# Four layers of graph networks with residuals on one core: W2·a kept in PSUM for the dots, and layer 3's statistics from ScalarE's sums

## The chip, the core and the metric

The kernel runs on one core of a Trainium2 chip. A core has five engines that work side by side, each through a queue of its own: TensorE (PE in the profile; its weight loads, PEld, overlap its products), VectorE (DVE), ScalarE (ACT), GpSimd (POOL) and SyncE (SP, which only starts transfers here). Data lies in SBUF; TensorE writes its results into PSUM, of which the kernel has eight banks of 128 partitions x 512 floats. Engines wait for each other only where one needs what another has written, or a buffer that another still reads.

The metric is the device time of one execution, in microseconds (us). The kernel before takes 2239.06 us, the median of three executions (2235.84 to 2239.59).

## The reference

The input x has 128 batches of 128 nodes with 512 features, all in fp32. Each of four layers adds its output to x and normalises over the features. Shapes and weights' names are cut here; `LN` is the normalisation without weights.

```python
# layer 0
y = einsum('nm,bmd->bnd', adj, x)
x = LN(x + einsum('bnd,do->bno', y, weight) + bias)
# layer 1
q, k, v = x @ Wq.T, x @ Wk.T, x @ Wv.T
rel = adj.T * einsum('bnd,bmd->bnm', q, k)
rel = rel / norm(rel, axis=2)
x = LN(x + einsum('bnm,bmd->bnd', rel, v))
# layer 2
h = x @ W                                # W is W2 in the kernel
s1, s2 = h @ a[:512], h @ a[512:]
e = leaky_relu(s1[:, :, None] + s2[:, None, :], 0.2) * adj
x = LN(x + elu(softmax(e) @ h + beta * h))
# layer 3: A = adj x, C = adj x + b, so C - A = b
out = max over the features of relu(A + b)      # one number per node
x = LN(x + out)
```

## The kernel before

**Tiling.** Four batches make a group, and there are 32 groups (G and NG). All four layers of a group are done on the core, so a group is loaded once and stored once. Large products, of 512 nodes x 512 by 512 x 512, are done with seven half-size products instead of eight (lines 290 to 362): y's product with layer 0's weights, m = x·(Wqᵀ·Wk) and v in layer 1, z in layer 2. Each of them runs seven steps in the order 1, 2, 6, 5, 7, 3, 4, and a step is eight matmuls of 256 columns. The running sums live in three PSUM tiles, r0, r1 and r2, each as large as a bank: r0 opens at step 1, r1 at step 2, r2 at step 5 (REGION, line 291). After a step its sum is read out, by a ScalarE copy or by a VectorE addition: in m, the copies are tT<-r_m after steps 1, 6, 5 and 4, and the additions tT<-r_m,tT after steps 2, 7 and 3. GpSimd makes the sums of left factors that the steps need (s_y, s_x, s_z; lines 294 to 311).

**Order.** Every engine runs in exactly the order in which the program names its instructions (InOrder, lines 18 to 26; since this helper records every operation, all rows of the profile say L26). The order is written out by hand: every piece of work has a due time, in 28 slots per group (TABLE, lines 231 to 246), and the pieces of all groups are sorted by due time (line 783) before they are emitted. A piece of group g that is due at 51.7 lies at 28·g + 51.7, so the four layers of neighbouring groups run interleaved: while layer 2 of a group is done, layer 0 of a later one is. FIRST (line 248) and LAST (lines 250 to 279) give other times to the first two and the last three groups.

**Around the change.** wa holds two rows, W2·a1 and W2·a2, spread over all partitions in SBUF (lines 138 and 202 to 212): since h·a = x·(W2·a), the reference's s1 and s2 are dot products of x rows with wa. VectorE does these dots on the unnormalised x2, two for each batch (line 559, scr<-x,wa, with the sum as a second output), and scale_dots (line 574, the instructions d) corrects them with the mean and the inverse deviation of the normalisation. Then TensorE spreads d (p_s, line 617) and the attention of layer 2 begins. The residual of layer 1 ahead of the dots (line 545, x<-p_o,rn,x) is followed by its statistics (stats, line 368: bn_stats and bn_aggr on VectorE). norm (line 375) is: VectorE adds eps (ve), GpSimd takes the power -0.5 (rstd), VectorE makes -mean·rstd (nmean), and ScalarE applies x·rstd + nmean.

In layer 3 (line 747) TensorE makes p_a = adj·x for a batch (widen), VectorE takes its greatest value over the features (mx), adds b and clips at zero (top), ScalarE adds that number to x, and then the statistics of this sum come from VectorE (stats3) and the norm follows.

**Buffers.** PSUM has one pool with two rings of four banks (lines 80 to 83): "ps" for single-bank tiles (p_y, p_rel, p_o, p_s, p_eT, p_z, p_a) and "r" for r0, r1, r2 of all products and, in the last group, for c (line 700). A matmul that opens a tile waits until the tile four before it in its ring has been read.

Of the kernel before, what the change touches and what calls it, by code (L numbers as in the profile page):

```python
# [8 lines left out]
FP = mybir.dt.float32  # L9
AF = mybir.ActivationFunctionType  # L10
ALU = mybir.AluOpType
AX = mybir.AxisListType

EPS = 1e-5
# [15 lines left out]
def kernel(  # L30
# [33 lines left out]
    pe, dve, act, pool = (InOrder(tc, e) for e in (nc.tensor, nc.vector, nc.scalar, nc.gpsimd))  # L64
    sync = InOrder(tc, nc.sync)
    B, N, D = x.shape
    P = 128
# [3 lines left out]
    H = D // 2  # L71
    G = 4
# [3 lines left out]
    const = ctx.enter_context(tc.tile_pool(name="const", bufs=1))  # L76
    data = ctx.enter_context(tc.tile_pool(name="data", bufs=2))
    work = ctx.enter_context(tc.tile_pool(name="work", bufs=1))
    small = ctx.enter_context(tc.tile_pool(name="small", bufs=4))
    psum = ctx.enter_context(tc.tile_pool(name="psum", bufs=4, space=bass.MemoryType.PSUM))  # L80

    def bank(name):
        return psum.tile([P, D], FP, tag="ps", name=name)

    def on_all(row, n):

# [5 lines left out]
    x1, x2, x3 = {}, {}, {}  # L92
# [28 lines left out]
    b3_sb = const.tile([P, 1], FP)  # L121
    nc.sync.dma_start(b3_sb, b3.rearrange("(p o) -> p o", o=1))

    ident = const.tile([P, P], FP)
    make_identity(nc, ident)
    mhalf = const.tile([P, G], FP)
    dve.memset(mhalf, -0.5)

    adjT = const.tile([P, P], FP)
    pt = bank("p_adjT")  # L130
    pe.transpose(pt[:, :P], adj_sb, ident)
    act.copy(adjT, pt[:, :P])
# [2 lines left out]

    m_qk = const.tile([P, K, D], FP)
    wvT = const.tile([P, K, D], FP)
    wa = const.tile([P, 2, D], FP)
    wa_sum = const.tile([P, 2], FP)
    beta_i = const.tile([P, P], FP)  # L140
    beta_b = beta_i[:, None, :].to_broadcast([P, G, P])
# [21 lines left out]
    def prepare_qk(c):  # L163

        pm = bank(f"p_m{c}")
        for e in range(K):
            pe.matmul(
                pm,
                wq_sb[:, e, c * P : (c + 1) * P],
                wk_sb[:, e, :],  # L170
                start=(e == 0),
                stop=(e == K - 1),
            )
        act.copy(m_qk[:, c, :], pm)
        if c == K - 1:
            bw["m"] = weight_blocks(m_qk, "m")
# [9 lines left out]
    col = const.tile([P, 2, K], FP)  # L186
# [15 lines left out]
    def prepare_rows():  # L202

        for i in range(2):
            p = bank(f"p_wa{i}")
            for k in range(K):
                pe.transpose(
                    p[:, k * P : (k + 1) * P], col[:, i, k : k + 1].to_broadcast([P, P]), ident
                )
            act.copy(wa[:, i, :], p)  # L210
        dve.tensor_reduce(wa_sum, wa, AX.X, ALU.add, negate=True)
        dve.tensor_scalar(beta_i, ident, beta_sb, None, op0=ALU.mult)

# [6 lines left out]
    def emit(at, f, *args):  # L220
        pieces.append((at, lambda: f(*args)))

    def each(at, f):
        for b in range(len(at)):
            emit(at[b], f, b)

    def row(at, step, n=G):
        return [at + i * step for i in range(n)]
# [6 lines left out]
        move=row(20.5, 0.1), x_sums=row(25.3, 0.5), m=row(28, 1, 7), scores=row(36.5, 1),  # L235
        masked=[39.95], squares=[40.4], turn_rel=[40.3],
        move_rel=row(41.2, 0.1), inverse=[42.5], v=row(42, 1, 7), attend=row(50.6, 1),
        residual=row(51.0, 1), dots=row(54.2, 1.1), norm1=[55.2], scale=[58.8],
        apply1=row(65.4, 0.33),
        spread=[61.6], leaky=[62.0], weighted=[63.4], greatest=[64.3], exps=[64.4],  # L240
        divide=[65.8], turn_att=[68.6], with_beta=[69.0], gather=row(71.5, 1),
# [2 lines left out]
        widen=[98.7, 100.0, 103.6, 104.6], top=[99.1, 100.4, 104.0, 105.0],  # L244
        stats3=[99.8, 101.1, 104.7, 105.7], norm3=[106.2], apply3=row(107, 0.33), store=[108.5],
# [8 lines left out]
            stats3=[27.0, 29.9, 32.2, 35.8], norm3=[42.0], apply3=row(44.0, 0.8), store=[47.4],  # L254
        ),
        NG - 2: dict(
            scale=[5.6], apply1=row(24.3, 0.8), spread=[6.9], leaky=[7.4], weighted=[9.0],
# [4 lines left out]
            top=[73.7, 74.6, 78.0, 78.9], stats3=row(79.8, 0.9), norm3=[83.4],  # L262
            apply3=row(84.8, 0.8), store=[88.2],
# [3 lines left out]
            squares=[17.2], turn_rel=[17.1], move_rel=row(18.0, 0.1), inverse=[20.0], v=[16.7, 18.4, 21.0, 22.7, 25.3, 27.9, 30.5],  # L267
            attend=row(33.2, 0.86), residual=row(34.1, 1.65), norm1=[40.65], dots=row(40.7, 1.53),
            scale=[47.0], apply1=row(47.5, 0.8), spread=[48.9], leaky=[49.4], weighted=[51.0],
# [5 lines left out]
            top=[83.5, 84.4, 85.3, 87.0], stats3=[86.1, 87.9, 88.8, 89.7],  # L275
            norm3=[86.9, 88.7, 89.6, 90.5], apply3=[88.3, 90.1, 91.0, 91.9],
# [62 lines left out]
    def product(at, name, mul, s, w, c, fresh, begin=None):  # L339


        r = {}

        def step(i):
            if i == 1 and begin is not None:
                begin()
            where = REGION[i]
            first = i in (1, 2, 5)
            if first:
                r[where] = psum.tile([P, 2, H], FP, tag="r", name=f"r{where}_{name}")  # L350
            mul(r[where], s["f"][i], bw[w][i], first)

        def out(i):
            p, dst = r[REGION[i]], c(*BLOCK[i])
            if fresh and i in (1, 6, 5, 4):
                act.copy(dst, p)
            else:
                dve.tensor_tensor(dst, p, dst, ALU.add)

        for n, i in enumerate(ORDER):  # L360
            emit(at[n], step, i)
            emit(at[n] + 0.72, out, i)
# [5 lines left out]
    def stats(s, g, b, t):  # L368
        if b == 0:
            s["mv"] = small.tile([P, G, 2], FP, tag="mv", name=f"mv_{g}", bufs=6)  # L370
        st = small.tile([P, 6], FP, tag="st", name=f"st_{g}_{b}")
        dve.bn_stats(st, t)
        dve.bn_aggr(s["mv"][:, b, :], st)

    def norm(at, apply_at, s, g, t):

        n = G // len(at)

        def spread(i):
            sl = slice(i * n, i * n + n)  # L380
            ve = small.tile([P, n], FP, tag=f"ve{n}", name=f"ve_{g}_{i}")
            dve.tensor_scalar(ve, s["mv"][:, sl, 1], EPS, None, op0=ALU.add)
            s["r", i] = small.tile([P, n], FP, tag=f"rstd{n}", name=f"rstd_{g}_{i}")
            pool.tensor_tensor(s["r", i], ve, mhalf[:, sl], ALU.pow)

        def shift(i):
            sl = slice(i * n, i * n + n)
            s["nm", i] = small.tile([P, n], FP, tag=f"nmean{n}", name=f"nmean_{g}_{i}")
            dve.scalar_tensor_tensor(
                s["nm", i], s["mv"][:, sl, 0], -1.0, s["r", i], op0=ALU.mult, op1=ALU.mult  # L390
            )

        def apply(b):
            i, j = b // n, b % n
            act.activation(
                t()[:, b, :],
                t()[:, b, :],
                AF.Identity,
                bias=s["nm", i][:, j : j + 1],
                scale=s["r", i][:, j : j + 1],  # L400
            )

        each(at, spread)
        for i in range(len(at)):
            emit(apply_at[i * n] - 0.1, shift, i)
        each(apply_at, apply)
# [207 lines left out]
    def layer2(g, t):  # L614
        s = {}
# [83 lines left out]

        def direct(b):  # L700

            s["c", b] = psum.tile([P, D], FP, tag="r", name=f"c_{g}_{b}")
            for k in range(K):
                pe.matmul(
                    s["c", b],
                    s["zT"][:, k, b * P : (b + 1) * P],
                    w2_sb[:, k, :],
                    start=(k == 0),
                    stop=(k == K - 1),
                )  # L710
# [15 lines left out]
        n = G // len(t["exps"])  # L726
# [20 lines left out]
    def layer3(g, t):  # L747
        s = {}

        def widen(b):  # L750
            s["a", b] = bank(f"p_a_{g}_{b}")
            pe.matmul(s["a", b], adjT, x3[g][:, b, :], start=True, stop=True)

        def top(b):
            x = x3[g][:, b, :]
            mx = small.tile([P, 1], FP, tag="mx", name=f"mx_{g}_{b}")
            dve.tensor_reduce(mx, s["a", b], AX.X, ALU.max)
            tp = small.tile([P, 1], FP, tag="top", name=f"top_{g}_{b}")
            dve.tensor_scalar(tp, mx, b3_sb, 0.0, op0=ALU.add, op1=ALU.max)
            act.activation(x, x, AF.Identity, bias=tp)  # L760

        def store(i):
            for b in range(i * n, i * n + n):
                sync.dma_start(out[g * G + b], x3[g][:, b, :])

        n = G // len(t["store"])
        each(t["widen"], widen)
        each(t["top"], top)
        each(t["stats3"], lambda b: stats(s, f"3_{g}", b, x3[g][:, b, :]))
        norm(t["norm3"], t["apply3"], s, f"3_{g}", lambda: x3[g])  # L770
        each(t["store"], store)


# [2 lines left out]
    each(row(18.0, 0.1), prepare_v)  # L776
    each(row(29.2, 1.8), prepare_dots)
    emit(40.7, prepare_rows)
    emit(61.0, prepare_2)
    for g in range(NG):  # L780
        for layer in (layer0, layer1, layer2, layer3):
            layer(g, times(g))
# [31 lines left out]
```

## Time and profile before

The profiled execution took 2236.61 us, and its span from first to last instruction is 2234.4 us. The mean granted TensorE clock is 0.996. The table gives busy time by stage: the filling of the pipeline, the main part with its regular groups, and the drain.

| stretch (us) | length | PE | DVE | ACT | POOL |
|---|---|---|---|---|---|
| 0 to 203 | 203.0 | 185.7 | 128.5 | 61.1 | 83.7 |
| 203 to 2100 | 1897.0 | 1887.1 | 1560.3 | 852.2 | 863.9 |
| 2100 to 2234.4 | 134.4 | 110.0 | 106.1 | 66.8 | 35.5 |

A busy time counts an instruction from start to end, so one that is held up by a neighbour in SBUF counts for longer. Groups of instructions are named by output and inputs: scr<-x,wa is the dot, tT<-r_m,tT an addition behind m's product. Some rows of the groups that the change touches (mean of one instruction, and the idle time of the engine right before it over the whole span):

| engine, instruction | count | mean ns | idle before, us |
|---|---|---|---|
| DVE mx<-p_a (128x512) | 128 | 677 | 7.6 |
| DVE top<-mx,b_sb | 128 | 215 | 4.6 |
| DVE mv<-st (bn_aggr) | 512 | 182 | 17.6 |
| DVE d<-mv,wa_sum,d | 64 | 450 | 0.0 |
| ACT x<-x,top (128x512) | 128 | 722 | 229.1 |
| ACT sq<-rel, square with sum (128x128) | 128 | 295 | 20.6 |
| ACT read of the accumulator behind it | 128 | 187 | 0.0 |
| POOL s_x<-xT (128x512 pieces) | 64 | 1497 | 256.5 |

### The profile page before, as it was taken

Reading aid. Unit: us, or ns where it says so; the run is one execution under the profiler, and the core shown is the slowest. Engines: PE = TensorE matmul, PEld = TensorE weight load, DVE = VectorE, ACT = ScalarE, POOL = GpSimd, SP = SyncE. Lnnn points to the kernel's source line nnn. Section 1 sums busy time; section 2 is a strip of 40 time slices with the busy share of each in tenths; the row PEclk is TensorE's granted clock in tenths of the full one; section 3 lists DMA queues with packets and bytes.
Section 4 is the critical chain, followed back from the end, with each engine's and each line's share of the span. In section 5 each row is a group of like instructions: output and inputs, shape, how many; then the busy total and the mean of one; then the engine's idle time right before and its main releaser. Section 6 shows DMA issues by size and latency. Waiting matters only on the chain.

```text
span 2234.4 us, 31661 instructions
## 1 busy us (share of the span) xinstructions
PE 2182.9 (98%) x11073; PEld 1842.1 (82%) x11073; DVE 1794.9 (80%) x3534; ACT 980.0 (44%) x1936; POOL 983.1 (44%) x743
## 2 busy tenths in 40 slices
PE   7999999999999999999999999999999999999996
PEld 5888888888888888888888888888888888888873
DVE  4668888778878788888788888788888788887788
ACT  2224444444444454444444444444344444444535
POOL 3435454435455344544344554344553354443322
PEclk9999999999999999999999999999999999999998
DMA  4010222211222211222201222202222112221101
GB/s 166 25 32 19 60 57 62 62 28 40 60 59 62 62 19 48 59 60 62 59 19 52 58 61 62 52 22 55 57 62 63 41 28 59 58 62 43 21 28 57
DMA packets 333294, 115.15 MB, mean 52 GB/s; under 512 B 297424, under 2 KB 297552, under 8 KB 333136
## 3 DMA queue, kind: packets, MB, share of 16 engines
q1 hardware_dynamic: 331936, 110.77, 19.6%
q10 hardware_dynamic: 1200, 2.36, 0.3%
q8 instruction: 89, 1.46, 0.3%
q14 instruction: 69, 0.57, 0.1%
HBM read 39.65 MB, written 33.55 MB: 33 GB/s over the span
## 4 chain that ended last, share of the span: by engine, by line
PE 75%; DVE 20%; issue 3%; POOL 1%; ACT 1%; DMA 0%; DVEq 0%; ACTq 0%; POOLq 0%
PE r_v L26 17%; PE r_y L26 15%; PE r_z L26 14%; PE r_m L26 8%; DVE scr L26 6%; DVE x L26 6%; PE p_z L26 5%; PE p_o L26 5%; PE p_a L26 5%; PE p_rel L26 4%; DVE st L26 2%; PE p_y L26 2%; DVE tT L26 1%; DVE d L26 1%; PE p_m L26 1%
## 5 line engine op out<-in xcount | busy, mean ns | idle before, releaser
L26 ACT ACTIVATE x<-x,nmean,rstd 128x512 f32<-128x512 f32 x512 | 385.8, 808 | 187.5 <-DVE nmean L26 187.4
L26 DVE BATCH_NORM_STATS2 st<-x 128x6 f32<-128x512 f32 x512 | 352.1, 688 | 56.7 <-ACT x L26 47.9
L26 DVE SCALAR_TENSOR_TENSOR scr<-x,wa 128x512 f32<-128x512 f32 x256 | 286.2, 1169 | 0.0
L26 POOL TENSOR_TENSOR rstd<-ve,mhalf 128x4 f32<-128x4 f32 (+1 forms) x134 | 145.2, 1083 | 286.9 <-DVE ve L26 280.7
L26 POOL TENSOR_TENSOR x<-x,bias_sb 128x512 f32<-128x512 f32 x128 | 193.2, 1519 | 76.9 <-PE p_y L26 76.4
L26 POOL TENSOR_TENSOR s_x<-xT 128x512 f32<-128x512 f32 x64 | 95.8, 1497 | 256.5 <-DMA xT<-xB 237.6
L26 ACT ACTIVATE x<-x,top 128x512 f32<-128x512 f32 x128 | 92.4, 722 | 229.1 <-DVE top L26 228.8
L26 DVE TENSOR_TENSOR x<-r_y,x 128x512 f32<-128x512 f32 x224 | 151.4, 676 | 27.1 <-PE r_y L26 27.0
L26 ACT COPY c<-r_z 128x512 f32<-128x512 f32 x124 | 71.8, 579 | 221.5 <-PE r_z L26 221.5
L26 ACT COPY yT<-p_y 128x512 f32<-128x512 f32 x128 | 75.1, 587 | 206.5 <-PE p_y L26 206.5
L26 PEld LDWEIGHTS p_y<-adjT,x 128*128 128x128 f32 x1024 | 135.8, 195 | 13.1 <-ACT adjT L26 5.2
L26 DVE SCALAR_TENSOR_TENSOR x<-p_o,rn,x 128x512 f32<-128x512 f32 x128 | 95.9, 749 | 59.9 <-PE p_o L26 56.0
L26 PE MATMUL p_y<-adjT,x 128*128 128x128 f32 x1024 | 136.7, 278 | 6.4 <-ACT adjT L26 4.9
L26 PEld LDWEIGHTS p_z<-eT,x 128*128 128x128 f32 x1024 | 133.9, 192 | 8.4 <-DVE x L26 1.2
L26 DVE SCALAR_TENSOR_TENSOR x<-m,x 128x512 f32<-128x512 f32 x128 | 129.7, 1013 | 13.6 <-DVE x L26 0.9
L26 PEld LDWEIGHTS p_rel<-xT,tT 128*128 128x128 f32 x1024 | 134.1, 191 | 7.4 <-DVE tT L26 0.8
L26 POOL TENSOR_TENSOR s_z<-zT 128x512 f32<-128x512 f32 x31 | 39.3, 1267 | 224.0 <-ACT zT L26 224.0
L26 PE MATMUL p_rel<-xT,tT 128*128 128x128 f32 x1024 | 134.9, 275 | 0.6 <-DVE tT L26 0.6
L26 PE MATMUL p_z<-eT,x 128*128 128x128 f32 x1024 | 134.8, 275 | 0.4 <-DVE x L26 0.4
L26 PE MATMUL p_a<-x,adjT 128*128 128x512 f32 x256 | 131.2, 597 | 3.6 <-ACT x L26 1.9
L26 ACT COPY tT<-r_m 128x512 f32<-128x512 f32 x128 | 75.7, 591 | 132.9 <-PE r_m L26 132.9
L26 PE MATMUL p_o<-v,relT 128*128 128x512 f32 x256 | 130.3, 593 | 0.0
(119 smaller groups left out, 5008.6 us busy)
## 6 DMA issues: line engine op xcount, KB each, us to landing
out_dram<-x SPq DMA_DIRECT2D x128, 256.0 KB, 2.5
x<-in_x_dram SPq DMA_DIRECT2D x31, 1024.0 KB, 5.8
xT<-xB SPq DMA_DIRECT2D x480, 64.0 KB, 2.3
relT<-relB SPq DMA_DIRECT2D x512, 16.0 KB, 1.8
w_sb<-in_L_gnn_weight_dram ACTq DMA_DIRECT2D x1, 1024.0 KB, 5.9
x<-in_x_dram SPq DMA_DIRECT2D x4, 256.0 KB, 7.9
wq_sb<-in_L_gnn_Wq_dram SPq DMA_DIRECT2D x1, 1024.0 KB, 12.1
wk_sb<-in_L_gnn_Wk_dram SPq DMA_DIRECT2D x1, 1024.0 KB, 14.9
```

The costliest lines, as they stand in the source:

```text
L26: return lambda *args, **kw: self.tc.keep_in_program_order(op(*args, **kw))
```

## The change

Two things are done. First, the two rows of wa stay in PSUM, where TensorE's transposes write them, and are no longer copied to SBUF; a dot then reads x2 from SBUF and wa from PSUM. As wa takes two banks for good, the other six are dealt out anew: three for single-bank tiles, two for r0 and the last group's c, and one that r1 and r2 share. The due times of the dots, of layer 1's norm (ve and rstd) and of scale_dots in TABLE move: the dots from 54.2, 55.3, 56.4, 57.5 to 51.7, 53.8, 54.9, 55.6, norm1 from 55.2 to 54.6, scale from 58.8 to 57.2. With these times the dots of the first two batches stand between the residuals on VectorE, the remaining ones behind the last residual and its statistics, and on GpSimd rstd of layer 1 stands ahead of the last of the s_x sums. LAST keeps its times.

Second, layer 3's statistics leave VectorE. ScalarE squares x with a sum as second output (sq) ahead of the addition of top, makes top itself (Relu of mx + b), and takes the sum of x + top while it adds top. With mean = sum/512 and the mean of x alone, mean - top, the variance is sq/512 - (mean - top)². Five small VectorE instructions per group make it (spread), GpSimd raises it to -0.5, one more makes -mean·r (shift), and ScalarE applies as before. In the last group these small instructions come per batch.

The purpose of both is to take work from VectorE: for the dots the contention of two SBUF operands, for layer 3 the bn_stats passes over 128x512.

```diff
-    psum = ctx.enter_context(tc.tile_pool(name="psum", bufs=4, space=bass.MemoryType.PSUM))
+    psum = ctx.enter_context(tc.tile_pool(name="psum", bufs=1, space=bass.MemoryType.PSUM))
     def bank(name):
-        return psum.tile([P, D], FP, tag="ps", name=name)
+        return psum.tile([P, D], FP, tag="ps", name=name, bufs=3)
...
-    wa = const.tile([P, 2, D], FP)
+    wa = psum.tile([P, 2, D], FP, tag="wa", name="wa")
...
         for i in range(2):
-            p = bank(f"p_wa{i}")
             for k in range(K):
                 pe.transpose(
-                    p[:, k * P : (k + 1) * P], col[:, i, k : k + 1].to_broadcast([P, P]), ident
-                )
-            act.copy(wa[:, i, :], p)
+                    wa[:, i, k * P : (k + 1) * P],
+                    col[:, i, k : k + 1].to_broadcast([P, P]),
+                    ident,
+                )
...
-        residual=row(51.0, 1), dots=row(54.2, 1.1), norm1=[55.2], scale=[58.8],
+        residual=row(51.0, 1), dots=[51.7, 53.8, 54.9, 55.6], norm1=[54.6], scale=[57.2],
...
-                r[where] = psum.tile([P, 2, H], FP, tag="r", name=f"r{where}_{name}")
+                r[where] = psum.tile([P, 2, H], FP,
+                    tag="r0" if where == 0 else "r12", name=f"r{where}_{name}",
+                    bufs=2 if where == 0 else 1)
...
-            s["c", b] = psum.tile([P, D], FP, tag="r", name=f"c_{g}_{b}")
+            s["c", b] = psum.tile([P, D], FP, tag="r0", name=f"c_{g}_{b}", bufs=2)
...
+        def squares(b):
+            ...
+            scr = work.tile([P, D], FP, tag="scr3", name=f"scr3_{g}_{b}")
+            act.activation(scr, x3[g][:, b, :], AF.Square, accum_out=s["sq"][:, b : b + 1])
         def top(b):
...
-            dve.tensor_scalar(tp, mx, b3_sb, 0.0, op0=ALU.add, op1=ALU.max)
-            act.activation(x, x, AF.Identity, bias=tp)
+            act.activation(tp, mx, AF.Relu, bias=b3_sb)
+            act.activation(x, x, AF.Identity, bias=tp, accum_out=s["sum"][:, b : b + 1])
+        def spread(i):
+            ...
+            dve.tensor_scalar(s["mean", i], s["sum"][:, sl], -1.0 / D, None, op0=ALU.mult)
+            dve.tensor_tensor(d, s["mean", i], s["top"][:, sl], ALU.add)
+            dve.scalar_tensor_tensor(d, d, -1.0, d, op0=ALU.mult, op1=ALU.mult)
+            dve.tensor_scalar(s["sq"][:, sl], s["sq"][:, sl], 1.0 / D, EPS, op0=ALU.mult, op1=ALU.add)
+            dve.tensor_tensor(d, d, s["sq"][:, sl], ALU.add)
+            pool.tensor_tensor(s["r"][:, sl], d, mhalf[:, sl], ALU.pow)
+        def shift(i):
+            dve.tensor_tensor(s["mean", i], s["mean", i], s["r"][:, sl], ALU.mult)
...
+        for b in range(G):
+            emit(t["widen"][b] - 0.1, squares, b)
         each(t["top"], top)
-        each(t["stats3"], lambda b: stats(s, f"3_{g}", b, x3[g][:, b, :]))
-        norm(t["norm3"], t["apply3"], s, f"3_{g}", lambda: x3[g])
+        each(t["norm3"], spread)
+        for i in range(len(t["norm3"])):
+            emit(t["apply3"][i * n] - 0.1, shift, i)
+        each(t["apply3"], apply)
```

## The prediction

> **What bounds the kernel now.** I read the page's engine shares first, then the waits of TensorE, then the groups of VectorE, then the timeline of two neighbouring groups of the main loop. The page's first part, two waits of TensorE (total, times, longest, us), and rows of VectorE's groups (busy us, ns of one, idle before):
>
> ```profile
> PE 2182.9 (98%) x11073; PEld 1842.1 (82%) x11073; DVE 1794.9 (80%) x3534; ACT 980.0 (44%) x1936; POOL 983.1 (44%) x743
> ```
>
> ```profile
> PE r_m L26 <- DVE tT L26: 6.8, 5, 1.7
> ...
> PE r_y L26 <- DVE x L26: 4.4, 17, 0.4
> ```
>
> ```profile
> L26 DVE BATCH_NORM_STATS2 st<-x 128x6 f32<-128x512 f32 x512 | 352.1, 688 | 56.7 <-ACT x L26 47.9
> L26 DVE SCALAR_TENSOR_TENSOR scr<-x,wa 128x512 f32<-128x512 f32 x256 | 286.2, 1169 | 0.0
> ...
> L26 DVE SCALAR_TENSOR_TENSOR x<-p_o,rn,x 128x512 f32<-128x512 f32 x128 | 95.9, 749 | 59.9 <-PE p_o L26 56.0
> ```
>
> TensorE is busy nearly always, so only its gaps can be won. I measured them from the starts of successive matmuls: back to back these are 0.112, 0.216 and 0.429 us apart for 128, 256 and 512 columns. All starts at that pace give 2161.6 us. What exceeds it is 55.8 us: 12.8 before 67.7 us, 7.8 from there to 203 us, 19.2 in the main part to 2100 us, 16.0 after it. The rest of the span is 3.4 us before the first matmul and 13.6 after the start of the last. The main part's 19.2 us lie at two places, both behind VectorE: m's last step (5.8 us in 4 groups) and y's steps after the first score product (some 15 groups, near 0.9 us each). A group without a gap takes 66.8 us. The timeline of VectorE and TensorE (start, us, engine, instruction, and the wait before it), a group with a gap, then one without:
>
> ```profile
> 1052.03 1.74 DVE L26 SCALAR_TENSOR_TENSOR scr<-x,wa 128x512 f32<-128x512 f32 x1
> ...
> 1055.38 0.68 DVE L26 TENSOR_TENSOR tT<-r_m,tT 128x512 f32<-128x512 f32 x1
> ...
> 1061.40 0.67 DVE L26 TENSOR_TENSOR tT<-r_m,tT 128x512 f32<-128x512 f32 x1
> ...
> 1062.13 1.13 PE L26 MATMUL r_m<-xT,t_m 128*128 128x256 f32 x4 [1.28 <-DVE tT L26]
> ```
>
> ```profile
> 1118.24 1.89 PE L26 MATMUL r_m<-xT,m_qk 128*128 128x256 f32 x8
> ...
> 1123.48 1.89 PE L26 MATMUL r_m<-s_x,m_qk 128*128 128x256 f32 x8
> ...
> 1123.80 0.68 DVE L26 TENSOR_TENSOR tT<-r_m,tT 128x512 f32<-128x512 f32 x1
> ...
> 1128.10 0.69 DVE L26 TENSOR_TENSOR tT<-r_m,tT 128x512 f32<-128x512 f32 x1 [0.18 <-PE r_m L26]
> ...
> 1132.42 0.66 DVE L26 TENSOR_TENSOR tT<-r_m,tT 128x512 f32<-128x512 f32 x1
> ```
>
> The queue of dots (1.74 us each while GpSimd works) makes the three reads of r_m late. In the second group the second read starts when TensorE is ready for it, and nothing is lost.
>
> **What the Trainium skill says.** "SBUF — State Buffer", Who interferes with whom: a VectorE instruction with two SBUF inputs shuts out, and is shut out by, a GpSimd instruction that reads SBUF, for the whole instruction; with one SBUF input it does not contend. The trace agrees: a dot takes 0.68 us alone and 1.74 beside s_x or a bias addition, while tT<-r_m,tT, with a PSUM input, stays at 0.66 to 0.69 in the same stretches. "Perfetto Trace Analysis", Optimization Strategy: repeated bubbles on a saturated engine can mean too little PSUM for the next tile; the trace of before has none of that kind in its main part, but this change takes banks away.
>
> **The change part by part.** (1) The dots. With wa in PSUM a dot has one SBUF input. Its form is not in the trace; lower bound 0.68 (an uncontended dot), upper 0.75 (x<-p_o,rn,x, PSUM, SBUF and a pointer). I take 0.69. Eight per group: 8 x 1.12 = 8.9 us (286.2/32) become 5.5. The s_x sums on GpSimd, 1.27 alone and up to 1.79 contended, shorten too.
>
> (2) Their order. The dots of blocks 0 and 1 go between the residuals, into VectorE's idle time (0.9 us before each residual). Laid along the second group: residual 3 and its statistics end at 1115.1, ve and c<-r_z at 1115.9, four dots 1118.4, the three small d instructions by 1119.1, rstd from GpSimd included, since it now stands ahead of the last s_x. So VectorE waits for m's step 2, which ends at 1119.97, and its read ends near 1120.9 instead of 1124.5. The second read is on time in each group (1128.1), so the third ends at 1133.1 to 1133.4, as in the better groups of before. The main part's gaps shrink from 19.2 to about 2 us: -17.2.
>
> (3) PSUM. Eight shared slots become 3 for single banks, 2 for r0, 1 for r1 and r2 together, 2 banks for wa. I took from the trace, for each matmul that opens a tile, the end of the last read of the tile that would now stand in its place. Single banks: at least 4.2 us early in the main part. r0: 15 us. r1/r2: y's step 5 0.77, v's 2.6, z's 2.5, v's step 2 2.4, z's 4.3, all early. Two would be late with the old VectorE order: m's step 5 (1123.48) against the read that ended at 1124.48, -0.8 to -2.1 in all 28 groups; and y's step 2 (1133.45) against the third read, +0.4 in half the groups, -0.9 in the others. Part 2 makes the first 2.6 us early, and the second about 0.1 to 0.4. Behind a late step stand all matmuls, and nothing else hides it; so this is nil here with a bound of 0.5 us per group.
>
> (4) Layer 3 statistics. Off VectorE per group: 4 x (688 + 182 + 215) and ve, nmean: 4.9 us; on it: six small instructions at 0.15 to 0.25, 1.2 us. On ScalarE: four squares, four Relu, four accumulator reads. "ScalarE: Activation LUTs", What ACT_TABLE_LOAD costs, gives 0.186 us + 0.83 ns per element, 0.28 with a pointer, 0.09 overlap: an estimate of 0.61 per square; for 128 elements it gives 293 ns, and the trace has 295 (sq), and 0.2 to 0.3 per Relu. With 0.09 per read (seen behind sq) this is 4 x (0.61 + 0.25 + 0.18) = 4.2 us on an engine with 30 of 67 us busy. The copies of v and zT that TensorE needs stand behind 0.4 to 3 us of idle time; pair by pair (square, Relu, shift) they end within 0.1 us of before. Nil. The changed program loads one activation table, as before.
>
> (5) Start. The fourth wv transpose has to wait for a slot (a read that ends 2.06 us late in the old trace); ScalarE's copies pace this stretch, so about +0.5. The first group's m step 5 at 107.8 waits for VectorE until 109.8, since all residuals fall together there: +2.0; but 2.24 (p_s for d) and 1.52 (step 4) go, and 2.5 in the next group. Sum: -3.7.
>
> (6) End. VectorE's 8 statistics (7 us) go and ScalarE gets 8 squares, 8 Relu, 8 reads. From the applies of norm 2 on (2205.5, earlier by 1.5 through shorter dots), ScalarE has 8 x 0.71 + 2 x 0.55 + 8 x 0.61 + 8 x 0.25 + 8 x 0.72 + 8 x 0.71 = 25.2, with 1.2 idle: 2231.9, against 2231.3 in the trace. One wait of 1.1 at 2137 goes. Together -0.5; bounds -4 and +3.
>
> Sum: -17.2 - 3.7 - 0.5 = -21.4; 2239.1 - 21.4 = 2217.7, so 2218.
>
> **Rivals.** A: the single r1/r2 bank lets the GpSimd lock through. If elu's two SBUF instructions each meet a whole GpSimd sum (1.27), y's step 2 waits 0.3 to 0.5 in each group: 2218 + 30 x 0.4 = 2230. For it: the slack of 0.1 to 0.4; against it: the same pair cost 1.18 to 1.57 in both kinds of group. B, slower: a new wait per group takes the place of the old, either that read a full 1.3 us late or ScalarE's pairs holding up v's copies, of which the tightest leaves 0.9: 30 x 1.0 = +30, so 2248. For it: no spare bank; against it: 1 to 3 us of idle time ahead of those copies. C, no change: the dots shorten but the end turns ScalarE-bound at its upper bounds and half a microsecond per group comes back: 2218 + 15 + 3 = 2236.
>
> **How the numbers follow.** The forecast 0.71, A 0.16, C 0.06, B 0.07. Faster than 2234.6: forecast and A, 0.87; within 0.2%: 0.06; slower: 0.07. Range: from 2212 (all 19.2 won, -4 at both ends) to A with the end's +2: 2232.
>
> **What would show it.** Right: scr<-x,wa near 690 ns; s_x sums near 1.27; groups 66.8 us apart; no wait of r_m for tT; r_y for x nearly gone; a new wait of some 2 us near 108 us; ScalarE the last engine at the end. Wrong: r_m or r_y waiting each group for a read of tT (A, B), v<-r_v among TensorE's releasers (B), or dots that stay over 0.75.

## The result and the profile after

The changed kernel takes 2217.97 us, the median of four executions (2217.06 to 2220.68); the kernel before took 2239.21 us beside it. The ratio is 0.991, with a 95% interval of 0.9893 to 0.9928: faster by 21 us, just under 1%. The profiled execution of after took 2217.06 us, its span is 2214.6 us, and the mean granted clock is 0.996 as before.

First the page's engine shares, and then the same two entries of TensorE's waits (total, times, longest, us), of the changed kernel:

```profile
PE 2170.9 (98%) x11073; PEld 1839.6 (83%) x11073; DVE 1547.9 (70%) x3290; ACT 1102.5 (50%) x2446; POOL 907.7 (41%) x743
```

```profile
PE r_m L26 <- DVE tT L26: 4.4, 1, 4.4
...
PE r_y L26 <- DVE tT L26: 1.9, 2, 1.5
```

VectorE has lost 247 us of busy time (1794.9 to 1547.9), ScalarE has gained 122 and GpSimd has lost 75 without a change to its work. TensorE's share stays at 98%. The wait of r_m for tT came five times before and comes once now, and it is longer than any of the five; the 17 waits of r_y for x are gone. The groups of VectorE and of ScalarE after (busy us, mean ns of one, idle before):

```profile
L26 DVE BATCH_NORM_STATS2 st<-x 128x6 f32<-128x512 f32 x384 | 263.8, 687 | 8.8
...
L26 DVE SCALAR_TENSOR_TENSOR scr<-x,wa 128x512 f32<-128x512 f32 x256 | 161.5, 675 | 0.0
...
L26 DVE SCALAR_TENSOR_TENSOR x<-p_o,rn,x 128x512 f32<-128x512 f32 x128 | 95.8, 748 | 24.2 <-PE p_o L26 23.3
```

```profile
L26 ACT ACTIVATE x<-x,top 128x512 f32<-128x512 f32 x128 | 92.4, 722 | 4.2
L26 ACT ACTIVATE scr<-x 128x512 f32<-128x512 f32 x128 | 79.8, 623 | 0.1
...
L26 ACT ACTIVATE top<-mx,b_sb 128x1 f32<-128x1 f32 x128 | 37.6, 293 | 111.7 <-DVE mx L26 111.7
```

A dot takes 675 ns, where it took 1169. The idle time ahead of the residuals x<-p_o,rn,x has gone from 59.9 to 24.2 us: dots stand in it. On ScalarE a square (scr<-x) takes 623 ns and a Relu 293.

The timeline of a group of the main part (start, duration, engine, instruction, wait):

```profile
1109.90 1.89 PE L26 MATMUL r_m<-xT,m_qk 128*128 128x256 f32 x8
...
1111.90 0.69 DVE L26 TENSOR_TENSOR tT<-r_m,tT 128x512 f32<-128x512 f32 x1
...
1115.14 1.89 PE L26 MATMUL r_m<-s_x,m_qk 128*128 128x256 f32 x8
...
1119.76 0.69 DVE L26 TENSOR_TENSOR tT<-r_m,tT 128x512 f32<-128x512 f32 x1 [1.14 <-PE r_m L26]
```

Step 2's matmuls last from 1109.90 to 1111.79. Their read now begins 0.1 us later and ends at 1112.6, 2.5 us before step 5 takes the same bank at 1115.14. In the trace of before it ended 0.8 to 2.1 us after that point, in all 28 groups of the main part. The second read waits for TensorE, not the other way round.

The gaps of TensorE, measured as in the prediction from the starts of successive matmuls, show where the time went. A main part without any gap comes out at -2.0 by this measure (its pace is a median; in e2 and e4 below TensorE has no wait there at this value), so -1.4 means 0.6 us of gaps.

| gaps, us | before | after | difference |
|---|---|---|---|
| first matmul | 3.4 | 3.5 | +0.1 |
| to 67.7 us | 12.8 | 13.2 | +0.4 |
| 67.7 to 203 us | 7.8 | 8.4 | +0.6 |
| 203 to 2100 us | 19.2 | -1.4 | -20.6 |
| from there to the last start | 16.0 | 17.2 | +1.2 |
| after the last start | 13.6 | 12.1 | -1.5 |
| sum | 72.8 | 53.0 | -19.8 |

The sum is the difference of the two spans (2234.4 - 2214.6). Everything won lies in the main part, and the start has lost a little. There the first group stands out:

```profile
107.87 3.70 POOL L26 TENSOR_TENSOR x<-x,bias_sb 128x512 f32<-128x512 f32 x3
...
107.91 2.46 DVE L26 SCALAR_TENSOR_TENSOR d<-mv,wa_sum,d 128x4 f32<-128x4 f32 x2
...
110.47 1.12 DVE L26 TENSOR_TENSOR d<-d,rstd 128x8 f32<-128x8 f32 x1
111.52 0.68 DVE L26 TENSOR_TENSOR tT<-r_m,tT 128x512 f32<-128x512 f32 x1
112.25 2.97 PE L26 MATMUL r_m<-s_x,m_qk 128*128 128x256 f32 x8 [4.39 <-DVE tT L26]
115.02 1.78 PE L26 MATMUL p_y<-adjT,x 128*128 128x128 f32 x8
```

Three instructions on 4 or 8 numbers per partition last 3.6 us beside GpSimd's bias additions, the read of r_m's bank stands behind them, and TensorE waits 4.39 us. The prediction had this wait at 2.0.

### The profile page after: what moved, and what is told of

Read it like the earlier page. It is cut to its first block, busy times and chain, and to the rows that moved or that the text cites. A ratio compares the mean times of both kernels' runs of the same rounds, so it can differ in the third digit from the quotient of the medians.

```text
span 2214.6 us, 31863 instructions
## 1 busy us (share of the span) xinstructions
PE 2170.9 (98%) x11073; PEld 1839.6 (83%) x11073; DVE 1547.9 (70%) x3290; ACT 1102.5 (50%) x2446; POOL 907.7 (41%) x743
## 4 chain that ended last, share of the span: by engine, by line
PE 93%; DVE 3%; ACT 2%; POOL 1%; issue 1%; DMA 0%; ACTq 0%; DVEq 0%; POOLq 0%
PE r_y L26 17%; PE r_v L26 17%; PE r_m L26 17%; PE r_z L26 17%; PE p_z L26 5%; PE p_rel L26 5%; PE p_y L26 5%; PE p_o L26 5%; PE p_a L26 5%; DVE x L26 1%; ACT x L26 1%; DVE st L26 1%; PE p_eT L26 1%; PE p_m L26 1%; PE p_s L26 1%
## 5 line engine op out<-in xcount | busy, mean ns | idle before, releaser
L26 ACT ACTIVATE x<-x,nmean,rstd 128x512 f32<-128x512 f32 x384 | 288.6, 808 | 120.8 <-DVE nmean L26 120.8
L26 DVE BATCH_NORM_STATS2 st<-x 128x6 f32<-128x512 f32 x384 | 263.8, 687 | 8.8
L26 POOL TENSOR_TENSOR x<-x,bias_sb 128x512 f32<-128x512 f32 x128 | 170.1, 1331 | 137.9 <-PE p_y L26 137.5
L26 DVE SCALAR_TENSOR_TENSOR x<-m,x 128x512 f32<-128x512 f32 x128 | 114.4, 894 | 108.5 <-ACT m L26 98.5
L26 POOL TENSOR_TENSOR s_x<-xT 128x512 f32<-128x512 f32 x64 | 82.2, 1285 | 261.1 <-DMA xT<-xB 250.2
L26 POOL TENSOR_TENSOR rstd<-ve,mhalf 128x4 f32<-128x4 f32 (+1 forms) x99 | 98.5, 995 | 194.1 <-DVE ve L26 188.9
L26 DVE SCALAR_TENSOR_TENSOR scr<-x,wa 128x512 f32<-128x512 f32 x256 | 161.5, 675 | 0.0
L26 DVE STREAM_TRANSPOSE xB<-x 128x512 f32<-128x512 f32 x120 | 81.2, 696 | 108.7 <-ACT x L26 97.7
L26 DVE TENSOR_REDUCE mx<-p_a 128x1 f32<-128x512 f32 x128 | 88.3, 691 | 69.6 <-PE p_a L26 69.6
## 6 DMA issues: line engine op xcount, KB each, us to landing
wq_sb<-in_L_gnn_Wq_dram SPq DMA_DIRECT2D x1, 1024.0 KB, 12.3
wk_sb<-in_L_gnn_Wk_dram SPq DMA_DIRECT2D x1, 1024.0 KB, 15.1
```

The costliest lines, as they stand in the source:

```text
L26: return lambda *args, **kw: self.tc.keep_in_program_order(op(*args, **kw))
```

## The experiments

All ratios are against runs of the kernel before that were taken beside them on the same chip. The medians of before were 2236.87 us beside e1, e3, e4 and e5, 2238.53 beside e2, e6, e7 and e8, and 2236.68 beside e9 to e12.

| run | what it is | us | ratio (95% interval) |
|---|---|---|---|
| e1 | before + layer 3 on ScalarE | 2239.45 | 1.0013 (1.0005 to 1.0020) |
| e3 | before + moved due times | 2218.03 | 0.9918 (0.9904 to 0.9933) |
| e4 | before + wa in PSUM and its rings | 2211.92 | 0.9893 (0.9876 to 0.9909) |
| e5 | before + the rings alone | 2262.79 | 1.0120 (1.0105 to 1.0135) |
| e2 | changed, layer 3 back on VectorE | 2220.25 | 0.9918 (0.9905 to 0.9932) |
| e6 | changed, first group's scale late | 2214.18 | 0.9890 (0.9876 to 0.9903) |
| e9 | changed, without group 2's bias | 2215.32 | 0.9898 (0.9884 to 0.9913) |
| e7 | e4 + ScalarE's statistics in group 30 | 2211.63 | 0.9879 (0.9865 to 0.9892) |
| e8 | e7 + other bank for one c tile | 2212.06 | 0.9879 (0.9865 to 0.9893) |
| e12 | changed kernel again | 2218.97 | 0.9915 (0.9900 to 0.9930) |
| e11 | e4 again | 2212.30 | 0.9886 (0.9870 to 0.9903) |
| e10 | e8 + group 30's instructions later | 2210.16 | 0.9877 (0.9862 to 0.9891) |

And the gaps of their profiled executions, in the stages of the table above:

| run | to 67.7 | to 203 | to 2100 | to last start | after it |
|---|---|---|---|---|---|
| e1 | 13.0 | 7.0 | 20.4 | 18.8 | 12.7 |
| e3 | 12.3 | 5.2 | 6.9 | 14.1 | 14.1 |
| e4 | 14.3 | 3.0 | -2.0 | 18.0 | 11.5 |
| e5 | 14.1 | 11.4 | 38.1 | 20.5 | 11.5 |
| e2 | 14.3 | 8.4 | -2.0 | 19.6 | 11.5 |
| e6 | 13.9 | 3.2 | -1.4 | 18.6 | 12.5 |
| e9 | 15.0 | 3.4 | -1.4 | 18.6 | 12.4 |
| e7 | 12.9 | 3.0 | -2.0 | 18.5 | 11.5 |
| e8 | 15.1 | 3.0 | -2.0 | 17.1 | 11.3 |
| e12 | 14.7 | 8.4 | -1.4 | 18.5 | 11.9 |
| e11 | 14.9 | 3.0 | -2.0 | 18.5 | 11.0 |
| e10 | 12.5 | 3.0 | -2.0 | 18.1 | 11.4 |

The change has three parts that can stand alone: wa in PSUM with the new rings, the moved due times, and layer 3. The theory of the prediction was that the moved times win the main part and that shorter dots and the rings belong to it as means and price. The rival readings were that VectorE's load as a whole mattered, or that one part is enough. The first four runs put each part alone on the kernel before.

**e1, layer 3 alone.** The edit is the layer 3 part of the diff, nothing else.

> The kernel before with layer 3's statistics from ScalarE, and nothing else of the change (wa in SBUF, old rings, old due times). My theory: the gaps of the main part come from the queue of dots ahead of m's reads, and layer 3's work stands elsewhere in VectorE's order, so they stay: r_m still waits some 5 us for tT in 4 or 5 groups, and the time is 2236 to 2240 (within 3 us of before). Rival (VectorE's load as such makes it late, so anything taken off it helps): the gaps go as in the full change, 2220 to 2224.

It took 2239.45 us, 0.13% more than before. VectorE's busy time fell to 1687.8 us, but r_m waits for tT as before:

```profile
PE p_a L26 <- ACT x L26: 7.5, 3, 4.4
PE r_m L26 <- DVE tT L26: 6.9, 5, 1.7
```

The wait of r_m for tT is what it was (6.8 us in 5 waits). So 107 us less work on VectorE was worth nothing in the main part, whose gaps are 20.4 us (19.2 before). What is new is p_a waiting for ScalarE's x, 7.5 us against 1.9: gaps at the end grew by 1.9 us in sum (18.8 + 12.7 against 16.0 + 13.6).

**e3, the moved due times alone.**

```diff
-        residual=row(51.0, 1), dots=row(54.2, 1.1), norm1=[55.2], scale=[58.8],
+        residual=row(51.0, 1), dots=[51.7, 53.8, 54.9, 55.6], norm1=[54.6], scale=[57.2],
```

> The kernel before with the new due times of dots, norm1 and scale, and nothing else (wa in SBUF, old rings, old layer 3). My theory: the dots stay contended (mean over 1.0 us), so of the four moved ahead of the residuals only part fits into VectorE's idle time there; m's second read comes earlier by 1 to 2 us, and about half of the main part's 19.2 us of gaps goes: 2226 to 2234. Rival (the order alone is what pays, and PSUM is not needed): 2218 to 2222. Other rival (no room for contended dots between the residuals): no change, 2238 to 2242.

I was wrong here, and the rival was right: 2218.03 us, the time of the whole change. The groups of VectorE in e3:

```profile
L26 DVE SCALAR_TENSOR_TENSOR scr<-x,wa 128x512 f32<-128x512 f32 x256 | 296.4, 1202 | 0.0
...
L26 DVE SCALAR_TENSOR_TENSOR x<-p_o,rn,x 128x512 f32<-128x512 f32 x128 | 95.6, 747 | 23.7 <-PE p_o L26 22.8
```

The dots are as contended as ever (1202 ns), and still the gaps of the main part fall from 19.2 to 6.9 us, and no wait of r_m for tT is left there. The dots that moved run in the 36 us in which VectorE used to wait for p_o (59.9 to 23.7), and that is 1.1 us per group, which was enough. What stays are ten waits of r_y for x, 3.7 us in all.

**e4, wa in PSUM alone,** with the new rings that it needs. Due times and layer 3 are those of before.

> The kernel before with wa in PSUM and the new rings, but the old due times and the old layer 3. My theory: a dot takes 0.68 us, eight behind the last residual end 3.4 us earlier than before, which is more than the 0.8 to 2.1 us by which m's step 5 would have found the shared r1/r2 bank unread; so the main part has no gap of note, and the first group waits for m's step 5 less than in the changed kernel, since the three d instructions stand behind the read there: 2215 to 2222. Rival (the moved due times are needed, or the shared bank costs a wait in each group): r_m waits for tT 0.5 to 1.5 us in nearly every group, 2232 to 2265.

It took 2211.92 us, less than the whole change and less than I had expected. The main part has no gap at all (-2.0). Eight dots of 675 ns in a row behind the last residual, in the old order, are early enough for step 5 on the shared bank. In the first group m's read stands ahead of the d instructions in the old order. TensorE's timeline there:

```profile
109.68 1.99 PE L26 MATMUL r_m<-s_x,m_qk 128*128 128x256 f32 x8 [0.64 <-DVE tT L26]
```

The wait is 0.64 us and not 4.39.

**e5, the rings alone,** so that their price is seen: 3, 2 and 1 banks as in the change, two banks left idle, and wa still in SBUF.

```diff
-        return psum.tile([P, D], FP, tag="ps", name=name)
+        return psum.tile([P, D], FP, tag="ps", name=name, bufs=3)
...
-                r[where] = psum.tile([P, 2, H], FP, tag="r", name=f"r{where}_{name}")
+                r[where] = psum.tile([P, 2, H], FP, tag="r0" if where == 0 else "r12",
+                    name=f"r{where}_{name}", bufs=2 if where == 0 else 1)
```

> The kernel before with the new PSUM rings (3, 2 and 1 banks, two left idle), wa still in SBUF, old due times, old layer 3. It prices the rings alone. My theory: m's step 5 waits in every group for the read of its shared bank, by the 0.8 to 2.1 us taken from the trace of before (about 1.4), r_m for tT becomes the longest entry of TensorE's waits, and the 17 us of old gaps go in exchange, since TensorE comes later: 2239 - 17 + 28 x 1.4 = 2261, range 2250 to 2275. Rival (three plus two plus one banks are enough, the wait isn't there): 2236 to 2242.

It took 2262.79 us. TensorE's waits, and VectorE and TensorE in one group:

```profile
PE r_m L26 <- DVE tT L26: 38.8, 31, 4.9
```

```profile
1137.90 0.68 DVE L26 TENSOR_TENSOR tT<-r_m,tT 128x512 f32<-128x512 f32 x1
...
1138.63 1.99 PE L26 MATMUL r_m<-s_x,m_qk 128*128 128x256 f32 x8 [0.89 <-DVE tT L26]
```

Step 5 (1138.63) begins when the read of step 2 has ended, and r_m waits like this 31 times. The lateness read off the trace of before was the right price: 2261 expected from it. With contended dots in the old order, the rings cost 26 us net; with dots of 675 ns they cost nothing in the main part (e4). These rings with contended dots in the new order were not run.

**e2, the changed kernel without layer 3's part.**

> The changed kernel with layer 3's statistics back on VectorE (wa in PSUM, new rings and new due times stay). My theory: layer 3's statistics are worth nothing in the main part (run e1), so the main part has no gap here either and the time is that of the changed kernel within 2 us, 2216 to 2220. Rival (in the changed kernel the relief of layer 3 is what lets the shared r1/r2 bank through): r_m or r_y wait for tT in most groups and the time is 2225 to 2245.

2220.25 us, ratio 0.9918, against 0.991 and 0.9915 (e12) with layer 3: no difference that these runs can tell. No wait of r_m or r_y returned in the main part (-2.0). So the shared bank doesn't need layer 3's relief. At the end the gaps sum to 31.1 us against 29.3 and 30.4 in the two profiles of the changed kernel; together with e1 layer 3's part is worth somewhere between 2 us gained and 3 us lost.

**e6 and e9, the first group.** The second question was what the wait of 4.39 us is made of. e6 moves scale_dots of the first group behind the read of r_m. e9 leaves the order and takes GpSimd's neighbour away: it leaves out the four bias additions of group 2, so that group's output lacks its bias.

```diff
# e6
-    FIRST = {0: dict(turn=row(20.4, 0.3)),
+    FIRST = {0: dict(turn=row(20.4, 0.3), scale=[58.8]),
# e9
-        each(t["bias"], biased)
+        if g != 2:
+            each(t["bias"], biased)
```

> The changed kernel with one number moved: in the first group scale_dots is due at 58.8 again instead of 57.2, so its three d instructions stand behind m's read and not ahead of it. In the changed kernel these three take 3.6 us there beside GpSimd's bias additions (107.9 to 111.6), and TensorE waits 4.4 us for the read behind them. My theory: the wait at 108 us shrinks to about 0.8 and the time falls by 3.6 us, to 2213 to 2216. Rival (the eight dots themselves make the read late, as my prediction had it): the wait stays at 2 us or more and the time falls by under 2 us, 2216 to 2219.

> The changed kernel with GpSimd's four bias additions of group 2 left out (the bias of that group is missing from the output, nothing else). They are what GpSimd runs from 107.9 us on, beside the three d instructions of the first group. My theory: the d instructions are long because GpSimd holds SBUF; without the additions they take 0.2 us each (0.6 in all and not 3.6), TensorE's wait at 108 us falls from 4.4 to about 1.4, and the time by 3 us: 2214 to 2216. Rival (the d instructions are long in themselves there, or wait for rstd): the wait stays over 4 us and the time is 2217 to 2219.

e6 took 2214.18 us and e9 2215.32. The timeline of e6, then that of e9:

```profile
108.33 0.69 DVE L26 TENSOR_TENSOR tT<-r_m,tT 128x512 f32<-128x512 f32 x1
108.93 1.87 DVE L26 SCALAR_TENSOR_TENSOR d<-mv,wa_sum,d 128x4 f32<-128x4 f32 x2
...
109.07 1.99 PE L26 MATMUL r_m<-s_x,m_qk 128*128 128x256 f32 x8 [0.79 <-DVE tT L26]
```

```profile
109.52 0.35 DVE L26 SCALAR_TENSOR_TENSOR d<-mv,wa_sum,d 128x4 f32<-128x4 f32 x2
109.98 0.17 DVE L26 TENSOR_TENSOR d<-d,rstd 128x8 f32<-128x8 f32 x1
110.08 0.69 DVE L26 TENSOR_TENSOR tT<-r_m,tT 128x512 f32<-128x512 f32 x1
...
110.83 1.99 PE L26 MATMUL r_m<-s_x,m_qk 128*128 128x256 f32 x8 [1.36 <-DVE tT L26]
```

In e9 the same three instructions, in the same place, take 0.6 us from the first's start to the read (109.52 to 110.08) without the bias additions beside them; with them it is 3.6 us (107.91 to 111.52). Their length is GpSimd's doing, and most of the wait is theirs: it comes down to 1.36 us here, and to 0.79 in e6, where they run just as slowly (1.87 for two) but behind the read. Some 0.8 us remain. In e4, too, 0.64 remain with the d instructions behind the read, so I put them down to what else stands ahead of it, the residuals and the eight dots; no run takes these away.

**e11 and e12, the parts against the whole on one chip.**

> The changed kernel itself, beside the next two on the same chip. Expected from its first runs: 2218, with the wait of 4.4 us at 108 us.

> Run e4's kernel once more (wa in PSUM and the new rings, old due times, old layer 3), beside the full change on the same chip. My theory: the other two parts of the change cost 4 to 6 us on top of this one, nearly all of it in the first group: 2210 to 2214. Rival (the difference between the two was one of chips): the same time as the changed kernel within 2 us.

2218.97 us for the whole change and 2212.30 for wa in PSUM alone: the moved due times and layer 3 cost 6.7 us on top of it. By the gap tables 5.4 of them lie between 67.7 and 203 us (8.4 against 3.0), in the first group, and 0.6 in the main part. e2, which has no layer 3 on ScalarE, loses the same 5.4 there, so the moved due times cost it.

**e7, e8 and e10, the end of e4.** In e4 VectorE works without a break at the end while ScalarE has time. These three look for what layer 3's part might be worth there.

```diff
# e7: ScalarE's version of layer 3 for one group, VectorE's for all others
+    def layer3(g, t):
+        (layer3_scalar if g in (NG - 2,) else layer3_vector)(g, t)
# e8, besides
-            s["c", b] = psum.tile([P, D], FP, tag="r0", name=f"c_{g}_{b}", bufs=2)
+            s["c", b] = psum.tile([P, D], FP, tag="r12" if b == 2 else "r0",
+                name=f"c_{g}_{b}", bufs=1 if b == 2 else 2)
# e10, besides, for group NG - 2
-            norm3=[83.4], apply3=row(84.8, 0.8)
+            norm3=[84.5], apply3=row(85.5, 0.8)
```

> The kernel with wa in PSUM and new rings, old due times, old layer 3 (as e4), but ScalarE's statistics in group 30 alone, the last but one. In e4 VectorE is busy nearly without a break from 2189 to 2204.6 us, with 3.5 us of group 30's statistics ahead of group 31's maxima, and ScalarE has 7 us of idle time in 2186 to 2198. My theory: layer 3's ScalarE part pays only where VectorE sets the end; p_a's wait for mx (4.9 us in e4) goes down to under 2 and the end comes 3 us earlier than in e4: 2207 to 2210. Rival (ScalarE becomes the engine that ends last, as in the changed kernel): 2211 to 2214.

> As e7, and the last group's third c tile takes the bank of r1/r2, which no product needs any more, instead of waiting for the first c tile's read (1.8 us at 2179 us in e4). My theory: this wait goes, but the elus behind it are paced by VectorE, so it brings 0 to 1.5 us beyond e7: 2206 to 2209. Rival (TensorE sets the pace there): 1.8 us in full.

> As e8 (wa in PSUM, old due times, ScalarE's statistics in group 30 alone, c's third tile in the idle bank), with group 30's small VectorE instructions behind two of group 31's maxima instead of ahead of them; in e7 they held the maxima up for 2.1 us by waiting for ScalarE. My theory: another 1 us, and 2 to 3 us below e11 beside it: 2208 to 2211. Rival (ScalarE sets the pace of these microseconds whatever VectorE does): as e11 within 1 us.

e7 took 2211.63 and e8 2212.06 us: both are above what I had expected, and neither is told from e4 by its interval. VectorE in e7:

```profile
2195.27 0.17 DVE L26 TENSOR_SCALAR mean<-sum 128x4 f32<-128x4 f32 x1 [2.15 <-ACT x L26]
```

The work taken off VectorE came back as a wait of 2.15 us for ScalarE's sums, with group 31's maxima queued behind it. e10 moves these small instructions back, and its time, 2210.16 us, is 2.1 us below e11 beside it, the best of this study (ratio 0.9877 to before). But its profile doesn't bear the theory out: from 2100 us on the gaps of e10 and e11 sum to the same 29.5 us, and the two spans differ in the start, which varied between 12.3 and 15.1 us among all these kernels. That e10 is better than e4 is not shown.

## Why the prediction was right, and where it was not

The time was met (2218 for 2217.97), partly by luck: two of its steps missed in opposite directions, and the kernel before was slower beside this result than beside the later runs. With the medians beside e12 the gain is 17.7 us and not 21.2.

**Step 1, the dots,** held: 0.69 taken, 0.675 measured. The reason held too. With one SBUF input the dots are no longer stretched, and GpSimd's sums are relieved in turn: s_x<-xT,s_x went from 1722 to 1290 ns. This agrees with the Trainium skill, "SBUF — State Buffer", Who interferes with whom, by which a VectorE instruction with only one SBUF input does not contend with GpSimd.

**Step 2, the order,** had about the right gain, but gave it a sole cause that it does not have. It forecast 17.2 us for the main part, and 20.6 came; part of the difference is the measure's own zero of -2.0, which I had taken for gaps that stay. But the step credited the moved due times, with the short dots as an aid. e3 and e4 show that either is enough for most of it: the order alone brings 12.3 of the main part's 19.2 us, the short dots alone all of it. They don't add up, since both bring VectorE's work forward at the same places. The working had the number that says so: eight dots fell from 8.9 to 5.5 us, 3.4 us earlier, more than the 2.1 us of the latest read.

**Step 3, the rings at nothing in the main part,** held as a sum, and e5 confirms the lateness read from the trace. Its reasoning has the same fault: it made the bank early by the moved order (2.5 us of margin at 1115.14, as forecast), where the short dots do it alone. The first form of rival B, a wait per group for the late read, is what e5 shows when the dots stay long in the old order. Rival A's wait, at y's step 2, is bounded by the 0.6 us of gaps that the whole main part has left.

**Step 4, layer 3 at nothing in the main part,** held within 0.6 us: in e1 its relief won nothing, and the main part's gaps are 0.6 us with ScalarE's statistics in all groups (the changed kernel, e6, e9, e12) and none without them (e2, e4). ScalarE's terms were a square of 0.61 us (0.623 measured) and a Relu of 0.2 to 0.3 (0.293). The estimate from "ScalarE: Activation LUTs", What ACT_TABLE_LOAD costs, is borne out by both.

**Step 5, the start at -3.7,** failed: it was +1.1. The waits that it saw go, for d and in the next group, did go. Three things went otherwise.

The first is the term "waits for VectorE until 109.8 ... +2.0". It priced the three d instructions ahead of the read as small ones. Beside GpSimd's additions they took 3.6 us, which e9 shows to be contention: the rule that the prediction itself quotes for the dots, two SBUF inputs against a GpSimd instruction that reads SBUF, holds for a 128x4 instruction as well, and its price is what is left of GpSimd's instruction, not a share of its own length. So the wait was 4.4 us. This price could be read before: in the trace of before the same three stand behind the read, beside GpSimd's sums s_y (113.33 and 114.67 us, 1.26 each), they take 3.1 us, and TensorE waits for them:

```profile
112.78 1.84 DVE L26 SCALAR_TENSOR_TENSOR d<-mv,wa_sum,d 128x4 f32<-128x4 f32 x2
114.72 1.23 DVE L26 TENSOR_TENSOR d<-d,rstd 128x8 f32<-128x8 f32 x1
...
116.10 0.83 PE L26 MATMUL p_s<-ident,d 128*128 128x128 f32 x4 [2.08 <-DVE d L26]
116.72 3.44 PE L26 MATMUL r_m<-xT,t_m 128*128 128x256 f32 x8
```

The second is "1.52 (step 4) go", which was no wait. It is the last of these lines: the eight matmuls of step 4 took 3.44 us instead of 1.89, at a granted clock of 0.50 from 116.4 to 119.8 us. In the changed kernel step 4 runs at full pace, but the same half clock comes a little earlier, behind the new wait (113.1 to 116.5 us), and costs 1.7 us there (last section). So it moved, and nothing was won by it.

The third is TensorE's next wait, 1.5 us of r_y for tT, which was not in the sum. It is in e4 and in e5 too (1.5 in each) and not in the kernel before, so it belongs to the rings. The forecast of 0.5 us for wv's slot can't be told: up to 67.7 us the gaps grew by 0.4, in a stretch that varied from 12.3 to 15.1 us among these kernels.

**Step 6, the end at -0.5,** came to -0.3. ScalarE is the last compute engine, as forecast (its last five applies end at 2211.5 of 2214.6). From the first apply of norm 2 to there it took 27.2 us, 24.3 before and 26.4 by the forecast (whose terms for its work sum to 25.1, not 25.2); the end's time ahead of that shrank by a little more.

**The sum.** In spans it is -20.6 + 1.1 - 0.3 = -19.8; between the medians it is 21.2, as the profiled execution of before was 2.6 us below the median. The miss of 4.8 us at the start and the excess of 3.4 us in the main part cancelled for the most part.

## What to carry to other kernels

Ask of each part of a change whether another part already cures the same wait: here moved due times and dots that don't contend both brought the same work of VectorE forward, and the second to arrive brought nothing but its own price in the first group. Load taken off VectorE where TensorE waits for none of it was worth nothing here, and it was 107 us (layer 3, e1). Before moving a tiny instruction with two SBUF inputs ahead of a critical read, look at what GpSimd runs beside it, and in the pipeline's first groups too: in the main part's group above GpSimd pauses between its additions, and the three d instructions take 1.3 us; in the first group three additions stand in a row. And before counting slow matmuls of the old trace as a wait that goes, look at the granted clock there.

## What the runs showed of the hardware that was not expected

A 128x4 or 128x8 VectorE instruction with two SBUF inputs takes 0.17 to 0.22 us alone and 1.1 to 1.3 us beside GpSimd's 128x512 additions of 1.27 us (e9 against the changed kernel). Each of the three in the first group ends within 0.02 us of the end of an addition: the neighbour sets its length.

A long wait can cost TensorE more than itself. The busy times by stretch of the changed kernel around the wait at 108 us (the stretch and its length; busy us and instructions of PE, PEld, DVE, ACT and POOL; then the granted clock, the DMA share and GB/s):

```profile
104.00:107.80 3.80, 3.80 (x26) 3.43 (x24) 3.70 (x11) 0.58 (x1) 2.15 (x2) 1.00 0.53 141
112.25:115.00 2.75, 2.75 (x8) 2.23 (x9) 0.00 (x0) 0.00 (x0) 0.00 (x0) 0.66 0.00 0
115.00:116.60 1.60, 1.60 (x9) 1.58 (x8) 0.00 (x0) 0.00 (x0) 0.00 (x0) 0.52 0.00 0
116.60:121.00 4.40, 4.40 (x25) 3.88 (x25) 2.33 (x3) 1.07 (x2) 4.04 (x3) 1.00 0.00 0
```

Behind the wait of 4.39 us the clock falls. The stretches above mix the two paces; taken alone, 113.1 to 116.5 us has a granted clock of 0.50, which is 3.4 us. Eight matmuls of m take 2.97 us instead of 1.99 (e6, e9), and eight of p_y 1.78 instead of 1.05: 1.7 us more. It was the same in e12. After waits of 0.8 and 1.4 us (e6, e9) the same matmuls run at full pace. But the kernel before also falls to 0.50, from 116.4 to 119.8 us, and there the wait was 2.08 us. The Trainium skill describes such a fall in "TensorE: Matmul & The Clock Gate", Part 1: The HAM clock gate (the "warmup" mystery): after an idle window of about 3.4 us the clock is halved until TensorE has been busy as long again. The 3.4 us at half clock agree with this in both traces. The idle time does not: 2.08 us were enough in the kernel before, and in e1 the same wait of 2.09 us is followed by full clock. So the length of one wait doesn't decide alone, and these runs leave open what does. Here a wait of 2 us or more could bring 1.7 us on top of itself.
